# Layers 1 and 2 in program order: columns among the three-tap products, spectra taken once and copied with signs among the frequency products, group statistics in the stage before

## The chip, the cores and the metric

The kernel runs on one core of one Trainium2 chip. A core has a matrix engine (TensorE, PE in the profile, with its weight loads shown apart as PEld), a vector engine (VectorE, DVE), a scalar engine (ScalarE, ACT), a general engine (GpSimd, POOL) and a sync engine that here issues DMAs (SyncE, SP). Each engine works through a queue of its own in order, and semaphores tie the queues together. Matrix products land in PSUM, which has eight banks of 128 x 512 f32; everything else stands in SBUF, 128 partitions wide. The metric is the time of one execution on the chip in microseconds; the median of several runs is given, and one further execution is profiled.

## The reference, cut to what matters

The input x is (2, 128, 64, 64) in f32: two images of 128 channels. Four layers each add something to x, after a group normalisation with 32 groups of 4 channels:

```python
def _gn(v, G=32, eps=1e-5):          # mean and variance of 4 channels x 64 x 64
    ...
x = x + _L0_conv_ref(_gn(x), ...)    # layernorm, 1x1 to 5C, depthwise 3x3, two attentions, 1x1, layernorm, 1x1
x = x + _L1_conv_ref(_gn(x), ...)    # convolutions and a correlation over columns, below
x = x + _L2_conv_ref(_gn(x), ...)    # product of spectra, below
x = x + _L3_conv_ref(_gn(x), ...)    # attention of 8 heads over 4096 positions
```

Layer 1:

```python
xp = jnp.pad(x, ((0, 0), (0, 0), (0, 0), (6, 6)))
t1 = jnp.stack([xp[..., 2 * k:2 * k + w] for k in range(7)], axis=2)
t2 = _conv(x, w2, (0, 1))                                    # 1x3, C to C: the three taps
t3 = jnp.einsum('nakhw,nbhw->nakb', t1, x) / math.sqrt(h * w)
t4 = ...                                                     # t2 shifted by -3..3 rows
t9 = p9w * (p6w * t3)
t7 = _conv(t2, w7, (0, 2), groups=c)
t8 = _conv(x, w8, (4, 4), dilation=(2, 2), groups=c)
t10 = jnp.einsum('nakb,nakhw->nbhw', t9, t4) / math.sqrt(c * 7)
return t8 - (t10 - t7)
```

Layer 2 splits the channels in four parts of 32 (a quaternion), takes the two-dimensional real spectrum of each, multiplies at each of 64 x 33 frequencies with 32 x 32 complex matrices, combines with signs, and goes back:

```python
Xs = jnp.fft.rfft2(xs, s=(64, 64), axes=(-2, -1))
Ws = jnp.stack([kr_w + 1j * ki_w, kr_x + 1j * ki_x, kr_y + 1j * ki_y, kr_z + 1j * ki_z])
C = jnp.einsum('piohw,qbihw->pqbohw', Ws, Xs)
Pw = C[0, 0] - C[1, 1] - C[2, 2] - C[3, 3]
Px = C[0, 1] + C[1, 0] + C[2, 3] - C[3, 2]
Py = C[0, 2] - C[1, 3] + C[2, 0] + C[3, 1]
Pz = C[0, 3] + C[1, 2] - C[2, 1] + C[3, 0]
o = jnp.fft.irfft2(P, s=(64, 64), axes=(-2, -1))
```

So part r of the result takes, with each part p of the weights, part r XOR p of the spectrum, with a sign that depends on r and p.

## The kernel before

**Order.** x stays in SBUF as `X`, 128 channels x 2 images x 4096 positions, from the first layer to the last. Instructions are written in Python; a framework assigns buffers, adds the waits that the buffers demand, and may move an instruction ahead of others of its engine by its own idea of what is due. The context `_in_order(tc)` takes that freedom away: within it each instruction of PE, DVE, ACT and POOL follows the one written before it on its engine. Before the change layer 1, layer 3, and the convolutions, the start and the end of layer 0 stand in it; layer 2 does not. Where two streams of work are to mix, one is a Python generator that is stepped between the steps of the other. DMAs are issued by SP, in their order.

**Statistics.** `_group_stats` (L123 to L143) has eight `bn_stats` on DVE, one per 512 positions, `bn_aggr`, a PE product with a 128 x 128 averaging matrix for the means (L130), three small DVE operations, a second product for the variances (L138), a square root on ACT (L140) and a reciprocal on DVE. Another form, `_group_stats_pow` (L1200 and on), takes the power -1/2 on POOL instead; layers 0 and 3 use it. Both are called at the start of the layer whose input they describe.

**Layer 0.** `normalize(b)` (L1289) normalises an image in eight tiles of 512 positions: ACT applies the group normalisation, PE transposes, `spread` takes the variance over channels on DVE (L1277, L1279), a maximum and an addition on DVE (L1196) and a power on POOL (L1197), and `scaled` multiplies on DVE (L1286). `finish(b)` (L1616) does the like at the end of the layer, with the output products (L1625, L1630) and the addition to `X` (L1641). In both, `scaled` of one tile stands ahead of `spread` of the next in program order. `convolutions` (L1440) computes pointwise (L1339) and depthwise (L1361) convolutions in eight parts n = 0 to 7; for the second image, `finish` of the first is stepped within its parts 0 and 1. Copies from PSUM are shared out in turn between ACT and DVE (`in_place`, L1372).

**Layer 1.** `padded(b)` computes statistics and normalises an image into a padded frame `g`. `columns(g)` gathers eight columns of `g` at a time (ACT, L569), transposes them (PE, L572) and copies them to `xt` (ACT, L577); `convolved(g)` does the three taps (PE, L590, copied by ACT, L597); `correlated(xt)` is 64 products for `t3` (PE, L605, the record count in the chain). The order is both images padded, columns 0, taps 0, columns 1, correlation 0, taps 1, correlation 1. Then `on_tiles` (PE, L644) and `combined` (PE, L673) are worked through for each image, while DVE adds the taps of the dilated 5 x 5 convolution (L625).

**Layer 2.** Its front goes over 16 groups of four columns of each image: DVE normalises (L147), PE transposes (L774), ACT copies (`gt`, L780), PE multiplies with the matrix `fwd_h`, DVE copies to `y` (L793). `y` holds the transform along rows for 33 frequencies m, both images. The products go over eight blocks `kb` of four frequencies m each. A block has a direct half (rows 4 kb + 1 to 4 kb + 4 of the weights) and a mirror half (the rows at the other end of the spectrum, whose spectra are taken from the same transform). For each half two weight tiles of 2.1 MB are loaded (`rows_of_weights`, five buffers), and `products` does, for 33 frequencies, four partition-wide products with the real and four with the imaginary weights, of 16 columns each (L875; 264 in a half, two matmul records each), into two PSUM banks, copied out as `pz` (L885). What is multiplied is `e`, one tile for a half: at partition block p, row m, result part r, image b, it holds spectrum part r XOR p with its sign. `spectra(kb)` fills both tiles of a block: for each m and image one 128 x 512 product with the constant `perm`, a matrix of 1 and -1 that transposes, permutes and signs in one (PE, L819); a copy of 128 x 512 (`yt`, ACT, L827); four products of 128 x 198 (PE, L842); four copies of 128 x 198 (DVE, L851). `turned` (L897, L904) transposes `pz` of a half; `back` (L920, L923) takes a block back along columns. They and `spectra` of the next block are generators: `alongside(products, side, steps)` steps them between the 33 frequencies of a half. Because the layer is not in `_in_order`, the profile shows the spectra in one bunch rather than spread. At last the layer goes back along rows, 16 groups for each image (L982, L988, an addition to `X`).

**Layer 3** starts with loads of small constants on SP and statistics; its `folded(0)` prepares weights for image 0.

Of the kernel before, what the change touches and what calls it, by code (L numbers as in the profile page):

```python
# [29 lines left out]
def _blocks():  # L30
# [13 lines left out]

    sign = np.array([[1, -1, -1, -1], [1, 1, 1, -1], [1, -1, 1, 1], [1, 1, -1, 1]], f8)
    perm = np.zeros((128, 4, 4, 32))
    for r in range(4):
        for p in range(4):
            for i in range(32):
                perm[(r ^ p) * 32 + i, r, p, i] = sign[r, p]  # L50
    k["perm"] = perm.reshape(128, 512)
# [451 lines left out]


# [4 lines left out]
def _layer1(ctx, tc, X, a, cst, eps5):  # L509
# [20 lines left out]
    nc.sync.dma_start(p9.rearrange("p k c -> p (k c)"), a["L1_conv_p9w"].to_broadcast([128, 7 * C]))  # L530
    d7 = one.tile([128, C], F32, name="d7")
# [14 lines left out]
    def padded(b):  # L546
# [3 lines left out]
        mean, rstd = _group_stats(nc, two, bank, x, cst, eps5)  # L550
# [5 lines left out]
        for c in range(NCH):  # L556
            r = slice(c * ROWS, (c + 1) * ROWS)
            _normalized(nc, g[:, 4 + c * ROWS : 4 + (c + 1) * ROWS, 4 : W + 4], xi[:, r, :], mean, rstd)
        return g

    def columns(g):

        xt = two.tile([128, 32 + 6, C], F32, name="xt")
        nc.gpsimd.memset(xt[:, 0:3, :], 0.0)
        nc.gpsimd.memset(xt[:, 35:38, :], 0.0)
        for u in range(0, 32, 4):
            gw = two.tile([128, 8, H], F32, name="gw")
            w0 = 4 + 2 * u
            nc.scalar.copy(gw, g[:, 4 : H + 4, w0 : w0 + 8].rearrange("p h w -> p w h"))  # L569
            pt = bank()  # L570
            for i in range(4):
                nc.tensor.transpose(  # L572
                    pt[:, i * 128 : (i + 1) * 128],
                    gw[:, 2 * i : 2 * i + 2, :].rearrange("p w h -> p (w h)"),
                    ident,
                )
            nc.scalar.copy(xt[:, 3 + u : 7 + u, :].rearrange("p u c -> p (u c)"), pt)  # L577
        return xt

    def convolved(g):  # L580
# [5 lines left out]
        for c in range(NCH):  # L586
# [11 lines left out]
        return t2  # L598
# [94 lines left out]
    xt = [columns(g[0])]  # L693
    t2 = [convolved(g[0])]
    xt.append(columns(g[1]))
    t3 = [correlated(xt[0])]
    t2.append(convolved(g[1]))
    t3.append(correlated(xt[1]))
    some(taps(0, g[0]), 42)
    t9 = [weights(*x) for x in t3]  # L700
    rest = taps(1, g[1])
    for b in range(B):
        for c in range(NCH):
            if c % 4 in (0, 2) and c < 4:
                z = on_tiles(g[b], t2[b], c // 2)
                some(rest, 4)
            ps = combined(t9[b], t2[b], c)
            some(rest, 2)
            added(b, c * CH, ps)
            if c in (1, 3):  # L710
                added(b, c // 2 * S // 2, z)

# [4 lines left out]

def _skewed(first, second, n, depth=1):

    waiting = []  # L720
    for i in range(n + depth):
        if i < n:
            waiting.append((i, first(i)))
        if i >= depth:
            second(*waiting.pop(0))
# [3 lines left out]
def _layer2(ctx, tc, X, a, cst, src, eps5):  # L729
    nc = tc.nc  # L730
    one = ctx.enter_context(tc.tile_pool(name="l2_one", bufs=1))
    wpool = ctx.enter_context(tc.tile_pool(name="l2_w", bufs=5))
# [26 lines left out]
    with tc.tile_pool(name="l2_a", bufs=3) as ap, tc.tile_pool(  # L759
        name="l2_aps", bufs=4, space=PSUM  # L760
    ) as aps:
        for b in range(B):
            x = X[:, b, :]
            xw = x.rearrange("p (h w) -> p w h", w=W)
            mean, rstd = _group_stats(
                nc, ap, lambda: aps.tile([128, CH], F32, tag="pt", name="ps_stat"), x, cst, eps5
            )

            def columns(i):
                g = ap.tile([128, 4, H], F32, name="g")  # L770
                _normalized(nc, g, xw[:, 4 * i : 4 * i + 4, :], mean, rstd)
# [8 lines left out]
                nc.scalar.copy(gt, pt[:, :256])  # L780
# [1302 lines left out]
```

## Time and profile before

| what | value |
|---|---|
| runs | 4671.17, 4682.22, 4674.94, 4677.45, 4668.28 us |
| median | 4674.94 us |
| profiled execution, own time | 4674.02 us |
| its span | 4672.2 us |
| mean granted TensorE clock | 0.931 of full |
| PE busy | 4295.3 us, 92% |
| ACT busy | 3265.4 us, 70% |
| DVE busy | 2118.6 us, 45% |
| POOL busy | 59.3 us, 1% |
| layer 0, by its last addition to X | 0 to 1682.7 us |
| layer 1, front (statistics to the last correlation) | 1682.7 to 1851.9 us |
| layer 1, tile convolutions and combinations, to the last on PE | 1851.9 to 1984.7 us |
| layer 2, front | 1985.4 to 2030.5 us |
| layer 2, block 0 to its direct products | 2030.5 to 2063.4 us |
| layer 2, mirror half 0 to direct half 7 | 2063.4 to 2542.3 us |
| layer 2, the rest | 2542.3 to 2649.6 us |
| layer 3 | 2649.6 us to the end |

The page has the busy time of every engine, the span in 40 slices with a digit for the busy tenths in each, the granted clock of PE and the DMA's share, and the chain of work that ended last, followed back from the last instruction. Further views list single instructions in order of time, with start and duration in microseconds, the engine, the line of the kernel, the operation, output and inputs, and in square brackets how long the engine was idle before and what released it. "x" counts records, and a piece of the chain can hold several. In the chain "issue" is time in which an engine waited for nothing that the profile shows.

### The profile page before, as it was taken

The page shows a single profiled execution, that of the slowest core. Times are in us where ns is not written, and L with a number is a line of the kernel's source. Part 1 is how long each engine was busy: PE and PEld are TensorE (multiplying, and loading weights), DVE is VectorE, ACT ScalarE, POOL GpSimd, SP SyncE. Part 2 cuts the span into 40 slices and gives each one's busy share as a digit, 9 for nine tenths or more (in the row PEclk, how much of TensorE's full clock was granted, in tenths as well). Part 3 has the DMA queues.
Part 4 walks back from the last instruction along what each step waited for, and adds up shares of the span by engine and source line. Part 5 has one row for each costly group of instructions (what it writes and reads, how often), then busy time and mean ns, then how long its engine had stood idle before and what let it go on. Part 6 is the DMA issues. An engine that isn't in the chain of part 4 may idle for free.

```text
span 4672.2 us, 95822 instructions
## 1 busy us (share of the span) xinstructions
PE 4295.3 (92%) x42698; PEld 1789.4 (38%) x42698; DVE 2118.6 (45%) x2192; ACT 3265.4 (70%) x3735; POOL 59.3 (1%) x141
## 2 busy tenths in 40 slices
PE   7899999889999968977676899999999999999998
PEld 3522222452222234466566733333333333333332
DVE  3689999458999986851121321131113211221111
ACT  3478888438888822221011289999999999999998
POOL 1000000000000010000000000000000000000000
PEclk9999999999999979986676589999999999999999
DMA  1000000000000000089876000000000000000000
GB/s 44 2 1 1 1 1 1 1 2 1 1 1 1 1 6 1 1 136 140 124 122 87 7 3 6 6 6 4 6 6 6 6 6 6 6 6 6 6 6 4
DMA packets 154267, 90.60 MB, mean 19 GB/s; under 512 B 24297, under 2 KB 148201, under 8 KB 153842
## 3 DMA queue, kind: packets, MB, share of 16 engines
q1 hardware_dynamic: 153842, 84.36, 11.1%
q8 instruction: 337, 5.52, 0.5%
q14 instruction: 88, 0.72, 0.1%
HBM read 75.94 MB, written 4.19 MB: 17 GB/s over the span
## 4 chain that ended last, share of the span: by engine, by line
PE 85%; DVE 6%; issue 5%; ACT 3%; POOL 1%; DMA 0%; SPq 0%; DVEq 0%; ACTq 0%; POOLq 0%
PE ps_acc L1884 22%; PE ps_s L1865 18%; PE ps_s L1166 12%; PE ps_acc L1570 11%; PE ps_sp L1361 3%; PE ps_freq L875 3%; PE ps_bank L673 2%; PE ps_pe L842 2%; PE ps_bank L819 1%; DVE sums L1605 1%; PE ps_t L605 1%; PE ps_sp L1339 1%; PE ps_po L994 1%; PE ps_bank L590 1%; PE ps_acc L1819 1%
## 5 line engine op out<-in xcount | busy, mean ns | idle before, releaser
L1875 ACT ACTIVATE weights<-ps_s 128x1024 f32<-128x1024 f32 x2048 | 1888.2, 1094 | 65.8 <-PE ps_s L1865 63.0
L1175 ACT ACTIVATE weights<-ps_s 128x1024 f32<-128x1024 f32 x1024 | 992.5, 1022 | 173.4 <-PE ps_s L1166 148.3
L1884 PE MATMUL ps_acc<-weights,vt 128*32 128x512 f32 x8192 | 1095.6, 607 | 0.0
L1865 PE MATMUL ps_s<-q,k 32*128 32x512 f32 x8192 | 933.1, 446 | 10.3 <-ACT weights L1875 10.3
L1605 DVE TENSOR_TENSOR sums<-sums,weights 128x2048 f32<-128x2048 f32 x384 | 879.1, 2289 | 42.4 <-ACT weights L1175 6.4
L1865 PEld LDWEIGHTS ps_s<-q,k 32*128 32x128 f32 x8192 | 473.8, 183 | 851.4 <-ACT weights L1875 792.1
L1166 PE MATMUL ps_s<-q,k 32*128 32x512 f32 x4096 | 646.2, 642 | 2.7 <-ACT weights L1175 1.3
L1570 PE MATMUL ps_acc<-weights,vt 128*32 128x512 f32 x4096 | 548.8, 605 | 3.4 <-ACT used L1595 3.2
L1906 DVE COPY u<-ps_acc 128x512 f32<-128x512 f32 x32 | 22.1, 692 | 1069.9 <-PE ps_acc L1884 1069.9
L1166 PEld LDWEIGHTS ps_s<-q,k 32*128 32x128 f32 x4096 | 210.0, 183 | 429.5 <-issue 212.4
L1884 PEld LDWEIGHTS ps_acc<-weights,vt 128*32 128x32 f32 x8192 | 163.1, 108 | 379.2 <-issue 367.2
L1570 PEld LDWEIGHTS ps_acc<-weights,vt 128*32 128x32 f32 x4096 | 81.0, 108 | 395.1 <-issue 377.0
L875 PE MATMUL ps_freq<-e,w_r 128*32 128x16 f32 x4224 | 143.4, 220 | 69.8 <-issue 69.4
L875 PE MATMUL ps_freq<-e,w_i 128*32 128x16 f32 x4224 | 141.4, 220 | 71.7 <-issue 71.7
L625 DVE SCALAR_TENSOR_TENSOR X<-g,w,X 128x2048 f32<-128x2048 f32 x84 | 197.3, 2350 | 2.4
L1605 DVE TENSOR_TENSOR sums<-weights 128x2048 f32<-128x2048 f32 x64 | 146.5, 2289 | 59.8 <-ACT weights L1175 59.8
L1361 PE MATMUL ps_sp<-pad,diag 32*32 32x512 f32 x4608 | 166.8, 607 | 4.0 <-DVE q L1372 3.3
L875 PEld LDWEIGHTS ps_freq<-e,w_r 128*32 128x32 f32 x4224 | 135.0, 159 | 76.3 <-issue 75.4
L875 PEld LDWEIGHTS ps_freq<-e,w_i 128*32 128x32 f32 x4224 | 134.2, 159 | 75.6 <-issue 75.5
L885 ACT COPY pz<-ps_freq 128x272 f32<-128x272 f32 x16 | 6.8, 424 | 213.0 <-PE ps_freq L875 213.0
L1826 DVE TENSOR_TENSOR vt<-ps_acc,bv 128x384 f32<-128x384 f32 x32 | 17.9, 558 | 295.4 <-PE ps_acc L1819 295.4
L885 DVE COPY pz<-ps_freq 128x256 f32<-128x256 f32 x16 | 6.8, 425 | 279.4 <-PE ps_freq L875 207.7
(278 smaller groups left out, 3200.9 us busy)
## 6 DMA issues: line engine op xcount, KB each, us to landing
w_r<-in_L_conv_kr_w SPq DMA_DIRECT2D x15, 528.0 KB, 12.1
w_r<-in_L_conv_kr_x SPq DMA_DIRECT2D x15, 528.0 KB
w_r<-in_L_conv_kr_y SPq DMA_DIRECT2D x15, 528.0 KB, 11.9
w_r<-in_L_conv_kr_z SPq DMA_DIRECT2D x15, 528.0 KB, 11.8
w_i<-in_L_conv_ki_w SPq DMA_DIRECT2D x15, 528.0 KB, 6.0
w_i<-in_L_conv_ki_x SPq DMA_DIRECT2D x15, 528.0 KB, 8.2
w_i<-in_L_conv_ki_y SPq DMA_DIRECT2D x15, 528.0 KB, 11.1
w_i<-in_L_conv_ki_z SPq DMA_DIRECT2D x15, 528.0 KB, 12.7
```

Source lines behind the costliest of these rows:

```text
L625: nc.vector.scalar_tensor_tensor(xi, g[:, i : i + H // 2, j : j + W], w8[:, s : s + 1], xi, ALU.mult, ALU.add)
L673: nc.tensor.matmul(ps.rearrange("p (h w) -> p h w", w=W), t9[:, k, :], t2[:, c * ROWS + k : (c + 1) * ROWS + k, 2 : W + 2], start=(k == 0) ...
L842: nc.tensor.matmul(pe[:, j * 6 * FW : j * 6 * FW + n * 3 * FW], yt[:, (r + j) * 128 : (r + j + 1) * 128], fwd_w[:, : n * 3 * FW], start=Tr ...
L875: nc.tensor.matmul(out.rearrange("p (x c) -> p x c", c=2), ws[n][:, :, s * FW + fw], e[:, s, :, :, 1 - n : 3 - n, fw].rearrange("p r b e - ...
L1166: nc.tensor.matmul(ps[j // 2][:, j % 2, :], k[rows, kt * 128 : (kt + 1) * 128], q[rows, qb * CH : (qb + 1) * CH], start=True, stop=True,)
L1175: nc.scalar.activation(w[:, 2 * p : 2 * p + 2, :], ps[p], AF.Exp)
L1361: nc.tensor.matmul(ps[r // 2][to, r % 2, :].rearrange("p (h w) -> p h w", w=W), diag[rows, grp, t, :], pad[rows, y0 : y0 + ROWS, t % 3 : t ...
L1570: nc.tensor.matmul(ac[n][rows, :], lhs(rows), w[:, j, :], start=first, stop=last)
L1605: nc.vector.tensor_add(parts[0].rearrange("p j c -> p (j c)"), t.rearrange("p j c -> p (j c)"), w.rearrange("p j c -> p (j c)"),)
L1865: nc.tensor.matmul(ps[j // 2][:, j % 2, :], k[rows, kt * 128 : (kt + 1) * 128], q[n][rows, qb * CH : (qb + 1) * CH], start=(n == 0), stop= ...
L1875: nc.scalar.activation(w[p], ps[p], AF.Exp)
L1884: nc.tensor.matmul(ac[0][32 * j : 32 * j + 32, :], vt[:, kt, j // 2, i : i + 2, :].rearrange("p a d -> p (a d)"), w[j // 2][:, i, :], star ...
```

## The change

Five things are changed together.

1. Layer 2 is put into `_in_order`. `spectra` drops the matrix `perm`: for each m both images are transposed into one bank, copied once (128 x 256), multiplied with `fwd_w` (two products of 128 x 198), and then copied 32 times (16 where only one half is wanted), a block of 32 partitions by 198 elements each, from part r XOR p to partition block p of `e`, with the sign as a factor: on ACT where p is even, on DVE where p is odd. Each r (four p) is a step of the generator, woven among the products of the mirror half. Of block 0 only the direct half's spectra are made ahead; the mirror half's are stepped among the direct products.
2. The front of layer 2 normalises on ACT with a scale and a shift, and copies `gt` on DVE.
3. Layer 1's `columns` and `convolved` become one function: gather group c + 1, then the three taps of row group c and the transposes of column group c.
4. The statistics of a layer's first image are computed in the layer before, as steps of a generator: layer 1's in layer 0's second convolutions, layer 2's among layer 1's combinations for the second image, layer 3's in the way back of layer 2. All use the power on POOL, so the square root on ACT goes. Layer 2's second image is stepped among the column groups of the first.
5. In layer 0's `normalize` and `finish`, `spread` stands ahead of `scaled`.

The diff, cut to its core:

```diff
 def _layer1(...)
+        if b or st is None:
+            st = two.tile([128, 2], F32, tag="st", name="st")
+            for _ in _stats_steps(nc, two, bank, x, cst, mhalf, st):
+                pass
...
-    def columns(g):
+    def columns_and_convolved(g):
...
+        def gathered(c):
+            gw = two.tile([128, 8, H], F32, name="gw")
+            w0 = 4 + 8 * c
+            nc.scalar.copy(gw, g[:, 4 : H + 4, w0 : w0 + 8].rearrange("p h w -> p w h"))
+            return gw
+
+        def worked(c, gw):
             ps = bank()
             ... # three taps of row group c, as before
             nc.scalar.copy(t2[:, 3 + c * ROWS : 3 + (c + 1) * ROWS, 2 : W + 2], pv)
-        return t2
+            pt = bank()
+            for i in range(4):
+                nc.tensor.transpose(pt[:, i * 128 : (i + 1) * 128], gw[:, 2 * i : 2 * i + 2, :]..., ident)
+            nc.scalar.copy(xt[:, 3 + 4 * c : 7 + 4 * c, :].rearrange("p u c -> p (u c)"), pt)
+
+        _skewed(gathered, worked, NCH)
+        return xt, t2
...
-    xt = [columns(g[0])]
-    t2 = [convolved(g[0])]
-    xt.append(columns(g[1]))
-    t3 = [correlated(xt[0])]
-    t2.append(convolved(g[1]))
-    t3.append(correlated(xt[1]))
+    xt, t2 = zip(*(columns_and_convolved(x) for x in g))
+    t3 = [correlated(x) for x in xt]
...
             some(rest, 2)
+            some(steps, 1)
...
+        if there is not None and b == 0:
+            steps = _stats_steps(nc, two, bank, X[:, 0, :], cst, mhalf, there)
...
 def _layer2(...)
+    ctx.enter_context(_in_order(tc))
...
             def columns(i):
                 g = ap.tile([128, 4, H], F32, name="g")
-                _normalized(nc, g, xw[:, 4 * i : 4 * i + 4, :], mean, rstd)
+                nc.scalar.activation(
+                    g, xw[:, 4 * i : 4 * i + 4, :], AF.Identity, bias=shift, scale=scale
+                )
+                next(steps, None)
...
-                nc.scalar.copy(gt, pt[:, :256])
+                nc.vector.tensor_copy(gt, pt[:, :256])
...
-                nc.tensor.matmul(pt, y[:, b, m, :, :].rearrange("p c w -> p (c w)"), k["perm"], ...)
-                yt = two.tile([128, CH], F32, name="yt")
-                nc.scalar.copy(yt, pt)
+                for b in range(B):
+                    nc.tensor.transpose(
+                        pt[:, b * 128 : (b + 1) * 128],
+                        y[:, b, m, :, :].rearrange("p c w -> p (c w)"),
+                        ident,
+                    )
+                yt = two.tile([128, B, 128], F32, name="yt")
+                nc.scalar.copy(yt.rearrange("p b i -> p (b i)"), pt[:, : B * 128])
...
+                for r in range(4):
+                    for p in range(4):
+                        to, of = slice(32 * p, 32 * p + 32), slice(32 * (r ^ p), 32 * (r ^ p) + 32)
+                        for s, e, row in places:
+                            out, x = e[to, row, r], got[of, :, s]
+                            if p % 2:
+                                nc.vector.tensor_scalar_mul(out, x, float(SIGN2[r][p]))
+                            else:
+                                nc.scalar.mul(out, x, float(SIGN2[r][p]))
+                    yield
...
-        es = []
-        for _ in spectra(0, es):
+        es = [None, None]
+        for _ in spectra(0, es, (0,)):
             pass
...
-            e = list(es)
-            side = iter(())
+            e, es = es, [None, None]
+            side = spectra(0, e, (1,))
             if before:
                 side = chain(turned(before[2][1], before[1]), back(kb - 1, before[0], before[1]))
-            alongside(products(rows_of_weights(kb, False), e[0], pz), side, 8)
+            alongside(products(rows_of_weights(kb, False), e[0], pz), side, 8 if before else 20)
             side = turned(pz[0], direct)
             if kb + 1 < BLOCKS2:
-                side = chain(side, spectra(kb + 1, es))
+                side = chain(side, spectra(kb + 1, es, (0, 1)))
             alongside(products(rows_of_weights(kb, True), e[1], pz), side, 24)
...
+def _stats_steps(nc, pool, psum_tile, x, cst, mhalf, got):
+    ...
     for c in range(NCH):
         nc.vector.bn_stats(st[:, c, :], x[:, c * CH : (c + 1) * CH])
+        if c % 2:
+            yield
...
     nc.vector.bn_aggr(mv, st)
+    yield
     pm = psum_tile()
     nc.tensor.matmul(pm[:, 0:1], cst["group"], mv[:, 0:1], start=True, stop=True)
...
+    yield
     pv = psum_tile()
     nc.tensor.matmul(pv[:, 0:1], cst["group"], e, start=True, stop=True)
+    _power(nc, pool, got[:, 1:2], pv[:, 0:1], 0.0, 1e-5, mhalf)
+    yield
...
 # layer 0, normalize
+            if 1 <= c < NCH + 1:
+                r[c - 1] = spread(turned[c - 1])
             if 2 <= c < NCH + 2:
                 y[c - 2] = scaled(turned[c - 2], r[c - 2])
-            if 1 <= c < NCH + 1:
-                r[c - 1] = spread(turned[c - 1])
...
 # layer 0, convolutions(pool, b, before)
+        if b == 1:
+            later = _stats_steps(nc, small, lambda: acc(0), X[:, 0, :], cst, mhalf, there)
...
+            if n in (3, 4):
+                for _ in range(4):
+                    next(later, None)
```

## The prediction

> **What bounds the kernel now.** The page first. Layers 0 and 3, the two attentions, fill most of the span, and the change hardly touches them. The granted clock and the DMA row mark layer 2: five slices of 0.5 to 0.8 clock with the DMA at 8 to 9 tenths. The chain is PE's nearly everywhere, with 5% of "issue".
>
> ```profile
> PE   7899999889999968977676899999999999999998
> PEclk9999999999999979986676589999999999999999
> DMA  1000000000000000089876000000000000000000
> PE 85%; DVE 6%; issue 5%; ACT 3%; POOL 1%; DMA 0%; SPq 0%; DVEq 0%; ACTq 0%; POOLq 0%
> ```
>
> Second, busy time by stretch for layer 2: its front, block 0, the seven further pairs of mirror and direct half, the last mirror half, the way back.
>
> ```profile
> 1985.40:2030.50 45.10, 31.84 (x200) 27.40 (x200) 41.33 (x91) 12.45 (x34) 0.00 (x0) 0.81 1.21 190
> 2030.50:2063.40 32.90, 27.60 (x608) 22.58 (x609) 10.57 (x33) 5.14 (x9) 0.00 (x0) 0.94 0.59 90
> 2063.40:2542.30 478.90, 337.60 (x8308) 286.23 (x8308) 87.19 (x252) 56.11 (x100) 0.00 (x0) 0.68 0.83 124
> 2542.30:2570.70 28.40, 20.76 (x577) 18.67 (x577) 2.20 (x5) 2.76 (x5) 0.00 (x0) 0.62 0.01 3
> ```
>
> Columns: stretch, length, then PE, PEld, DVE, ACT, POOL busy, clock, DMA share, GB/s. A pair takes 478.9/7 = 68.4 us, in which DVE works 12.5 and ACT 8.0: both have room, if they may use it. Third, the chain through one pair. The spectra stand in one bunch, PE alone from 2203.52 to 2222.42 (18.9 us). Products come in bursts of some 2.2 us with gaps put down to "issue", although nothing they read is late:
>
> ```profile
> 2187.22 2.23 PE ps_freq L875 x118
> 2189.45 6.18 issue
> 2195.63 2.21 PE ps_freq L875 x110
> 2256.13 2.18 PE ps_freq L875 x116
> 2258.31 6.23 issue
> ```
>
> About 128 matmuls with their 128 weight loads make a burst. The gap is 6.2 us while weights stream, 1.5 us when none do (block 0). A burst's period is so 8.4 or 3.7 us, whatever PE could do, and other work put between products is covered by it. Fourth, the start of layer 1:
>
> ```profile
> 1690.24 1.28 ACT L140 ACT_TABLE_LOAD   x1 [10.78 <-PE ps_bank L138]
> 1704.89 1.11 ACT L569 COPY gw<-g 128x512 f32<-128x512 f32 x1
> 1726.90 23.23 PE ps_bank L590 x48
> 1771.78 29.68 PE ps_t L605 x64
> ```
>
> T0 = 1682.69 ends layer 0. Up to 1726.9 PE is mostly idle: statistics, then columns of image 0, bound by ACT and PE in turn.
>
> **Layer 0.** In `normalize` and `finish` POOL's power (L1197, 1.02 us) and the hand-overs to it (some 0.1) stand on the chain, each tile once. The change lets DVE scale the previous tile (0.69) meanwhile. At the start 8 tiles gain at most 0.7 each: 5.6; I take -5 (-9 to -3). The first `finish`, inside the second image's convolutions, has a 3.8 us cycle over 8 tiles, but PE's own work there is some 3.5: -4 (-6 to -1). The last: -3 (-5 to 0). New in the second convolutions are the statistics for layer 1: eight `bn_stats` are 4.8 us of DVE (L126), and two small PE products (0.6 each) wait for DVE in PE's order with the fifth depthwise convolution (at 989.88) behind them: +4.5 (3 to 8). ACT's copies are queued behind no new wait. Sum: -7.5.
>
> **Layer 1.** Now image 0 is normalised at T0 (3.74 us), then the small scalings 2.0, `bn_stats` of image 1 4.84, aggregate 0.37, and the two PE products with DVE between them 1.9: PE may start convolving at T0+13. ACT's gathers (1.03), xt copies (0.59) and t2 copies (0.59) make 2.2 us per c. Beside them PE does a c's six matmul records (23.23/8 = 2.9) and transposes (1.13 at most), 3.3 to 4.0 in all, so ACT hides: eight times 3.3 is 26.2, for the first image 2.5 more to fill; correlations 57.2 (29.68 + 27.48). That ends at T0+125; now the tile convolutions (L644) start at 1851.93 = T0+169. So -44, or -43 with copies at the ends. Statistics of layer 2 among the last image's combinations: DVE lags PE there, and two products wait some 4: +4. Layer 1: -39 (-44 to -33). It is hidden nowhere: PE runs densely from 1851.93 to 1984.7.
>
> **Layer 2, front and end.** Without statistics (some 8 us for image 0), and with the normalisation moved to ACT and the gt copies to DVE, DVE keeps two operations per step, 0.37 and 0.60. 32 steps of 0.97, the other statistics 5.5 and the arrival of the constants 4.5 give about 41 against 45.1: -5 with the shorter constants (-8 to 0). SP's queue keeps its order, constants before weights, so the first weights are not later. The statistics at the end: two PE waits, +1. Layer 3 is held by its bias loads (2655.44, 2.89 us) anyway: -0.3; its Exp table load at 2700.55 (1.28) goes: -1.3. Sum: -5.6.
>
> **Layer 2, the spectra.** PE's work falls: per pair 8 times 2.2 us of 128x512 and 128x198 matmuls (L819, L842) become 4 times two transposes and two matmuls (some 1 us). The price is copies: 32 per m, of 32x198, ACT (L890) and DVE (L888) taking turns on one PSUM bank. Neither form is in the trace. By size ACT's copy lies between 0.22 (64 elements, L1346) and 0.373 (256, L780): 0.33. DVE's 128x198 copy is 0.36 alone, 0.32 to the next (L851): a pair is 0.68. Do the engines overlap? The nearest rows read another bank in quarters, ACT and DVE in turn:
>
> ```profile
> 945.36 0.68 DVE L1372 COPY q<-ps_sp 32x512 f32<-32x512 f32 x1 [9.50 <-ACT q L1372]
> 946.07 0.58 ACT L1372 COPY q<-ps_sp 32x512 f32<-32x512 f32 x1 [0.75 <-DVE q L1372]
> 946.68 0.69 DVE L1372 COPY q<-ps_sp 32x512 f32<-32x512 f32 x1 [0.64 <-ACT q L1372]
> ```
>
> Strictly one after the other, each waiting for the other's copy, 0.03 us between. The new copies have the same pattern: one tile read, one tile written, engines alternating. So an m costs 8 x 0.66 + 8 x 0.68 + 16 x 0.03 = 11.2 us, serially; four take 45. (With ACT's ends and DVE's 0.32 or 0.36 throughout, x is 9.1 to 12.2.) They are queued behind `turned` of the direct half: first copy about 8 us into the mirror half (5 to 11: last pz copy, eight transposes 1.9, two ACT copies, a fetch gap). The next direct half needs all of them, at 8 + 45 = 53. That half has 528 matmuls (8448 records in 16 halves), 4.1 bursts of 2.2 = 9, `turned` and the way back (1.9 + 7.0) between them, two or three short gaps and pz: 22 (19 to 25). Pair: 75.0 against 68.4, +6.6 seven times: +46. PE, the weights (0.83 of 68.4 = 57 us of transfer) and the gaps all fit beneath.
>
> Block 0: sixteen copies per m serially, 6.0; four and filling 2 give 26 where 18.6 was; then the mirror's spectra beside the direct products, 24 + 2.6 against 14.4. In all 52.6 against 32.9: about +19. The last mirror half and the way back stay.
>
> The page "PSUM — Partial Sum Buffer", section "PSUM bank collisions raise a hardware error", says that two engines may access one bank at once if their 32-partition quadrants differ. The copies of different p mostly qualify; by that rule alone they could overlap, and the first rival's sum would hold. The rows above do differ in quadrant and still go in turn, which shows an ordering that the program carries; I go by the rows.
>
> **Sum.** -7.5 - 39 - 5.6 + 46 + 19 = +13, on the profiled execution's own 4674.02 us: 4687. (It is 0.9 below the median 4674.94, so nothing is corrected.)
>
> **Rivals.** *First, the other side: the copies overlap or are short.* With x for an m's copies, a pair is 30 + 4x and block 0 is 8 + 4x, so layer 2's products change by 32x - 294: at x = 11.2 it is +65; it balances the -52 elsewhere at x = 10.8 and says faster by over 0.2% below 10.5. That is 0.02 us per copy, so this rival needs little. If the engines overlap fully, x = 16 x 0.34 = 5.5; the pair then meets its transfers at 57 to 59: -9.4 x 7 - 3 - 52 = -121, 4553. For: DVE's next copy starts earlier than its record ends (0.32 against 0.36), ACT has small copies of 0.22. Against: the rows above.
>
> *Second, slower still:* with the copies stretched over the mirror half, its matmuls of the next direct half no longer run ahead of the gaps, and the direct half meets full streaming: another 6.2 us gap per pair, 7 x 6.2 = 43: 4730. For: every gap with weights in flight is 6.2. Against: PE's mirror products end early, so the weights start earlier and are mostly there.
>
> *Third, the layer-1 gain is not there:* the convolutions wait for ACT's gathers in ACT's order, 2.2 us plus PE's transposes per c, as the columns do now (2.82 per c). Then PE works as slowly as before and only the statistics go, -20 instead of -39: 4706.
>
> *Fourth, as before:* with x near 10.8, 4674.
>
> The page "Runtime: NRT & Kernel Launch", section "Instruction fetch mechanics", says instructions come in blocks of 256 and their loading is mostly hidden. The gaps after each 256 here, 1.5 and 6.2 us, are not; were they hidden, a direct half would be some 12 us shorter before and after alike.
>
> **How the numbers follow.** What is uncertain is mostly layer 2: x by 0.7 gives 22, the direct half by 3 gives 21, the first copy by 3 gives 21, the rest 8; together about 32 either way; the ends of x alone, 9.1 and 12.2, would give 4620 and 4719. My forecast's kind (serial copies, x over 10.9) 0.54, first rival 0.20 (full overlap 0.06 of it), second 0.11, third 0.08, fourth 0.07. The bounds that leave out 2 in 10 are 4630 and 4745. A difference of 0.2%, 9 us, is about what a measurement of this kernel can tell from no change. Faster by more: the first rival and the forecast's lower spread, 0.31. Within: the fourth and what lies around it, 0.17. Slower: 0.52. The forecast's own range is 4660 to 4720.
>
> **What would show it.** Right: L890 and L888 in strict turns, each idle "<-" the other's e; PE idle at the first product of a direct half until the last e copy; a pair of about 75 us; convolutions of layer 1 from T0+13 and its tile convolutions at T0+125; no table load at the start of layer 1; a PE gap of 4 us ahead of the fifth depthwise convolution of image 1. Wrong: ACT and DVE busy with e at the same instant, a pair under 68, or a PE that waits for gw in layer 1. What would upset the sum most is the price of a 32x198 copy, since 128 of them stand in each pair's chain: 0.02 us each is 20 us in all.

## The result and the profile after

| | time |
|---|---|
| before, median of 44 runs | 4675.36 us (4667.29 to 4683.29) |
| after, median of 24 runs | 4681.66 us (4674.25 to 4689.55) |
| ratio after to before | 1.0012, 95% interval 1.0007 to 1.0018 |
| forecast | 4687 us, 4630 to 4745 |

The change costs 0.12%: measurable over this many runs, and inside the band of 0.2% that the prediction had called "the same" (chance given: 0.17; "slower": 0.52). The forecast was 5 us too high. That closeness is luck: two of its steps were wrong by 40 and 37 us, with opposite signs, and 5.5 us come from a stretch whose code is the same and whose difference no run explains.

The page of the kernel after, its slices and its chain:

```profile
PE   6999999789999979955465889999999999999998
PEclk9999999999999989976656589999999999999999
DMA  1000000000000000177976000000000000000000
PE 77%; DVE 13%; ACT 6%; issue 3%; DMA 0%; SPq 0%; POOL 0%; DVEq 0%; ACTq 0%; POOLq 0%
```

PE's share of the chain has gone from 85% to 77%, DVE's from 6% to 13%, ACT's from 3% to 6%: work that was PE's alone now ends on other engines. The stretches of layer 2 (columns as before: length, busy time of PE, PEld, DVE, ACT, POOL, clock, DMA share, GB/s), cut at the same events as in the prediction:

```profile
1977.40:2013.40 36.00, 29.71 (x196) 24.08 (x196) 32.42 (x81) 24.43 (x32) 0.55 (x1) 0.95 1.21 183
2013.40:2068.10 54.70, 25.07 (x585) 20.32 (x585) 23.50 (x65) 23.81 (x73) 0.00 (x0) 0.64 0.75 112
2068.10:2556.30 488.20, 274.66 (x7896) 232.48 (x7895) 159.14 (x477) 154.34 (x519) 0.00 (x0) 0.60 0.79 119
2556.30:2584.70 28.40, 21.64 (x578) 19.14 (x579) 2.20 (x5) 2.76 (x5) 0.00 (x0) 0.70 0.01 3
```

In the seven pairs PE is busy 63 us less than before (274.7 against 337.6), and the pairs still take 9.3 us longer (488.2 against 478.9). DVE and ACT work 72 and 98 us more.

A table by stage shows where the 6.2 us by which the profiled span is longer (4678.4 against 4672.2) come from. The events are the first or last instruction of the named lines in the two traces.

| stage | before | after | difference | forecast |
|---|---|---|---|---|
| layer 0, to the last addition to X | 1682.7 | 1715.0 | +32.3 | -7.5 |
| layer 1, to its last addition | 302.7 | 262.5 | -40.3 | -39 |
| layer 2, front | 45.0 | 35.9 | -9.1 | -5 |
| block 0, to the direct half's pz | 32.8 | 54.8 | +21.9 | +19 |
| seven pairs of mirror and direct half | 478.9 | 488.2 | +9.3 | +46 |
| last mirror half, way back | 107.8 | 108.4 | +0.6 | +1 |
| layer 3, start to its first Exp | 51.9 | 48.8 | -3.1 | -1.6 |
| layer 3, the rest and the end of the span | 1970.4 | 1964.9 | -5.5 | 0 |

### The profile page after: what moved, and what is told of

The parts are those of the page before. It is cut to its first block, busy times and chain, and to the rows that moved or that the text cites. A ratio compares the mean times of both kernels' runs of the same rounds, so it can differ in the third digit from the quotient of the medians.

```text
span 4678.4 us, 95586 instructions
## 1 busy us (share of the span) xinstructions
PE 4224.3 (90%) x42260; PEld 1731.8 (37%) x42260; DVE 2202.2 (47%) x2452; ACT 3386.2 (72%) x4212; POOL 66.1 (1%) x145
## 4 chain that ended last, share of the span: by engine, by line
PE 77%; DVE 13%; ACT 6%; issue 3%; DMA 0%; SPq 0%; POOL 0%; DVEq 0%; ACTq 0%; POOLq 0%
PE ps_acc L1953 22%; PE ps_s L1934 18%; PE ps_s L1215 12%; PE ps_acc L1636 11%; DVE X L644 4%; PE ps_sp L1420 3%; DVE e L888 3%; ACT e L890 3%; PE ps_freq L912 2%; DVE sums L1671 1%; PE ps_sp L1398 1%; PE ps_po L1032 1%; PE ps_acc L1888 1%; ACT weights L1224 1%; PE ps_bank L957 1%
## 5 line engine op out<-in xcount | busy, mean ns | idle before, releaser
L890 ACT ACTIVATE e<-ps_pe 32x198 f32<-32x198 f32 x512 | 144.1, 320 | 180.8 <-DVE e L888 163.4
L888 DVE TENSOR_SCALAR e<-ps_pe 32x198 f32<-32x198 f32 x512 | 166.6, 357 | 216.2 <-ACT e L890 216.0
L644 DVE SCALAR_TENSOR_TENSOR X<-g,w,X 128x2048 f32<-128x2048 f32 x84 | 197.3, 2350 | 2.4
## 6 DMA issues: line engine op xcount, KB each, us to landing
w_i<-in_L_conv_ki_y SPq DMA_DIRECT2D x15, 528.0 KB, 10.8
```

Of the source, the lines that this page charges most:

```text
L644: nc.vector.scalar_tensor_tensor(xi, g[:, i : i + H // 2, j : j + W], w8[:, s : s + 1], xi, ALU.mult, ALU.add)
L888: nc.vector.tensor_scalar_mul(out, x, float(SIGN2[r][p]))
L890: nc.scalar.mul(out, x, float(SIGN2[r][p]))
```

## The experiments

Each run is compared with the kernel before on the same chip. What is said of stages is from the traces, cut as in the table.

**1 and 2: the order in layer 0's `finish`.** The largest miss was layer 0. The last `finish` takes 59.3 us from the attention's last Exp to the last addition, against 43.2. Its cycle in the chain of the kernel after (start, duration, engine, what):

```profile
1671.12 0.89 DVE ln_st L1336 x4
1672.01 0.29 DVE ln_mv L1338 x4
...
1672.33 0.17 DVE ln_r L1245
1672.50 0.60 DVE y L1345
...
1673.24 0.75 PE ps_sp L1691 x4
1673.98 1.71 PE ps_acc L1696 x2
1675.69 0.43 PE ps_sp L1701 x2
...
1678.21 0.89 DVE ln_st L1336 x4
```

A tile now takes 7.1 us, and the chain goes through DVE and PE one after the other. Before, the same stretch had no PE in its cycle:

```profile
1660.95 1.02 POOL ln_r L1197
1661.99 0.69 DVE y L1286
1662.69 0.66 DVE X L1641
1663.35 0.80 DVE ln_st L1277 x4
1664.14 0.29 DVE ln_mv L1279 x4
...
1664.77 1.02 POOL ln_r L1197
```

The first experiment puts the old order back in `finish` alone, the second puts the new order alone into the kernel before.

```diff
 # experiment 1, against the kernel after (experiment 2: the reverse, against the kernel before)
-            if c < NCH:
-                r[c] = spread(ps[c])
             if 1 <= c < NCH + 1:
                 y[c - 1] = scaled(ps[c - 1], r[c - 1])
             if c >= 3:
                 ...
+            if c < NCH:
+                r[c] = spread(ps[c])
```

> The changed kernel with the order in finish put back (scaled of the tile before, the addition to X, then spread); normalize keeps its new order. Theory A, that the new order ties DVE and PE into one loop (spread of tile c waits for PE's products of c, these stand behind PE's transposes of tile c-2, which wait for a scaled that now stands behind the spread of c-1): the last finish goes from 55 us back to 39 (-16) and the first, inside the second image's convolutions, from 58.8 between its first and eighth addition back to 48 (-10.5), so 4681.7 - 26.5 = 4655. Theory B, that the lost time in layer 0 comes from the statistics newly put into the convolutions and the last finish is slow for another reason (PE's clock): no more than -5, 4677. The gap of 4 to 5 us before the fifth depthwise convolution stays in both.

> The kernel before with the new order in finish alone. Theory A: +16 in the last finish and +10 in the first, 4675.4 + 26 = 4701. Theory B (the order by itself is harmless or helps, as the prediction had it, -7): 4668 to 4675.

Measured: experiment 1 4650.2 us, ratio to before 0.9955 (0.9936 to 0.9974); experiment 2 4706.8 us, 1.0073 (1.005 to 1.0095). In experiment 1 layer 0 ends at 1687.0, 27.9 us earlier than after. Its last `finish` is 43.2 again and the first takes 49.8 instead of 58.8 from its first to its eighth addition. In experiment 2 layer 0 ends 33.0 us later than before; 16 of it in the last `finish`, 9.4 between the additions of the first, and 5.0 ahead of its first addition, which had not been counted, and 1.8 between the eighth addition and the second attention. Theory A holds from both sides: this one move costs some 28 to 34 us. Its old-order cycle, from experiment 1, has POOL's power on the chain again and is the quicker one:

```profile
1662.55 0.69 DVE y L1345
1663.24 0.66 DVE X L1707
1663.89 0.80 DVE ln_st L1336 x4
1664.70 0.29 DVE ln_mv L1338 x4
...
1665.32 1.02 POOL ln_r L1246
```

**3 and 4: the turns of ACT and DVE.** After the change every row m has its copies in strict turns. Some of them in order of time, ACT's (L890) and DVE's (L888) (start, duration, engine, line, operation, what, and in brackets the idle time and its releaser):

```profile
2242.75 0.55 ACT L890 ACTIVATE e<-ps_pe 32x198 f32<-32x198 f32 x2 [0.70 <-DVE e L888]
2244.02 0.55 ACT L890 ACTIVATE e<-ps_pe 32x198 f32<-32x198 f32 x2 [0.72 <-DVE e L888]
```

```profile
2243.33 0.65 DVE L888 TENSOR_SCALAR e<-ps_pe 32x198 f32<-32x198 f32 x2 [0.61 <-ACT e L890]
2244.59 0.62 DVE L888 TENSOR_SCALAR e<-ps_pe 32x198 f32<-32x198 f32 x2 [0.61 <-ACT e L890]
```

Each engine stands idle for as long as the other works. Experiment 3 gives all 32 copies of a row to one engine, experiment 4 gives all to DVE.

```diff
 # experiment 3
-                            if p % 2:
+                            if todo.index(m) % 2:
                                 nc.vector.tensor_scalar_mul(out, x, float(SIGN2[r][p]))
                             else:
                                 nc.scalar.mul(out, x, float(SIGN2[r][p]))
 # experiment 4
-                            if p % 2:
+                            if True:
```

> The changed kernel with the 32 signed copies of a row m all on one engine, ACT for even places in the block and DVE for odd ones, instead of ACT and DVE in turn by p. Theory A, that the turns make one chain of the copies (9.65 us per m, 38.6 per mirror half) and that this chain sets the pair: two chains run side by side, an m takes 32 x 0.32 = 10.3 us on its engine, four m take some 21 to 23; the pair goes from 70 to 55-60, where the weights' transfers (57 us per pair) stop it, -11 seven times, and block 0 loses two times 12: 4681.7 - 77 - 24 = 4581 (4570 to 4610). Theory B, that the engines can't read PSUM for these copies at once, or that instruction fetch or the transfers set the pair anyway: the period stays at 68 to 70, 4670 to 4690.

> The changed kernel with all signed copies on DVE. Theory A (in turns, two engines do no more than one): an m takes 32 x 0.32 = 10.2 us against 9.65, so +2.2 per pair, +15, and block 0's sixteen copies 5.1 instead of 5.9 per m, -6: 4681.7 + 9 = 4691 (4680 to 4700). Theory B (the engines do overlap in part): DVE alone is clearly longer, 13 us or more per m, +13 per pair, 4775 or more.

Experiment 3: 4654.8 us, 0.9962 (0.995 to 0.9974). Experiment 4: 4704.2 us, 1.0062 (1.0039 to 1.0084). In experiment 4 the seven pairs take 503.8 us, 15.6 more than after, as theory A had it: two engines in turns do hardly more than one of them alone. (The total is 13 us above its forecast and outside the range given. Block 0 did not become 6 us shorter: it takes 55.2 against 54.8. Layer 0, whose code is the same, ends 6.5 us later in that profile, and the front and layer 3 are longer by 2 and 5; such differences of 2 to 6 us between kernels in untouched stretches appear in several runs here and were not traced.)

Experiment 3 misses its forecast by 74 us. Two chains do run side by side (ACT and DVE copy into `e` at the same time for 79 us in all, against 14 in the kernel after) and block 0 falls from 54.8 to 39.8, but the seven pairs only go from 488.2 to 471.8. The chain of a mirror half with copies by row shows what has taken the place of the turns:

```profile
2209.74 0.50 PE ps_freq L912 x23
2210.24 4.09 issue
...
2216.64 1.62 PE ps_pe L874 x4
2218.26 0.73 PE ps_freq L912 x32
2218.99 4.01 issue
...
2224.19 1.63 PE ps_pe L874 x4
...
2225.85 0.62 DVE e L888 x2
...
2236.27 0.44 DVE pz L922
...
2239.59 5.55 issue
...
2248.45 5.09 issue
```

The products stand still in "issue" (experiments 6 and 7 say for what); the last spectra (L874) stand behind them in PE's order and come at 2224.2; the 32 copies of the last row follow for 10 us with nothing beside them. The direct half takes 28.1 us on average against 23.3 in the kernel after. The one shown has 29.8 with two long gaps, 5.55 and 5.09 us; in the kernel after the same half has 25.6, with one of 5.80 and one of 0.69.

**5 and 11: the spectra earlier among the products.** Experiment 5 takes experiment 3, the old order of `finish`, and steps the side work of a mirror half twice as fast. Experiment 11 is the same without the copies by row.

```diff
-            alongside(products(rows_of_weights(kb, True), e[1], pz), side, 24)
+            alongside(products(rows_of_weights(kb, True), e[1], pz), side, 48)
```

> The changed kernel with finish's old order, the copies by row (even places ACT, odd DVE), and the side steps of a mirror half stepped twice as fast (48 instead of 24 per half), so that PE's transposes and matmuls of the spectra come in the first half of the products and the copies of the last m end with the products, not 10 us behind. Theory A (in the run with copies by row the tail of the last m's copies is exposed): the mirror half falls from 40 to 31-33 us, the pair from 69.6 to 61, 7 x 8 = 56 less: 4654.8 - 27 - 56 = 4572 (4560 to 4595). Theory B (loading of PE's instructions while weights stream paces a pair, some nine blocks of 256 at some 7.5 us whatever stands between): pair 68 to 70, 4654.8 - 27 = 4628.

> The changed kernel with finish's old order and the mirror half's steps doubled, the copies still in turns. If the chain of 38.6 us per half is what counts, an earlier start gives only the time by which the first copy comes earlier, some 4 us of 12: pair 66 against 70, 4650 - 28 = 4622 (4610 to 4640). If the late weave alone was the fault, the pair falls to 61 as with copies by row: 4585.

Experiment 5: 4572.3 us, 0.9786 (0.977 to 0.9803), a version some 2% quicker than both kernels; its seven pairs take 424.8 us, 60.7 each. (That the total meets its forecast is in part luck: against experiment 3 the pairs gave 47 us and not 56, layer 0 gave 35 and not 27.) Experiment 11: 4653.3 us, 0.9959 (0.9945 to 0.9974), no gain over experiment 1 and outside both theories; its pairs take 70.9, and the expected 66 was wrong. The difference to experiment 5 is seen half by half. One mirror and one direct half, of the kernel after, of experiment 11 and of experiment 5, by stretch (columns as above):

```profile
2286.90:2331.80 44.90, 20.31 (x560) 16.26 (x560) 20.86 (x66) 20.33 (x71) 0.00 (x0) 0.61 1.00 155
2331.80:2356.70 24.90, 18.84 (x570) 17.06 (x568) 1.81 (x3) 1.57 (x3) 0.00 (x0) 0.51 0.48 74
```

```profile
2180.40:2223.80 43.40, 18.54 (x560) 15.25 (x560) 20.83 (x65) 20.30 (x71) 0.00 (x0) 0.65 0.95 148
2223.80:2251.60 27.80, 18.76 (x568) 17.02 (x568) 1.81 (x3) 1.56 (x3) 0.00 (x0) 0.50 0.57 86
```

```profile
2146.80:2177.70 30.90, 18.05 (x560) 14.90 (x560) 20.79 (x65) 20.43 (x71) 0.00 (x0) 0.72 0.95 146
2177.70:2208.50 30.80, 18.97 (x568) 17.14 (x568) 1.80 (x3) 1.56 (x3) 0.00 (x0) 0.51 0.90 139
```

With the turns the mirror half gains only 1.5 us from the earlier start, and more of the stream falls into the direct half (share 0.57 against 0.48), which grows by 3. In experiment 5 the DMA has a share of 0.95 of 30.9 and 0.90 of 30.8 us, which looks like 57 us of transfer in a pair of 61, the floor that the prediction's first rival had named (57 to 59). But a share of 1 is not the most there is: the front of layer 2 has 1.21 at 183 GB/s, against 138 over these pairs. At 183 GB/s the 8.4 MB of a pair (138 GB/s times 60.7 us) would take 46 us, an estimate from these rows. In a quarter of the time of these pairs less than 60 GB/s moves (in slices of 1 us), and SP waits there 156 us in 12 waits for products to free a buffer. So the transfers are not the bound of experiment 5.

**6 and 7: no weight stream.** Both leave out the loading of weights after block 0: the products of all blocks use block 0's weights. Experiment 6 has the turns, experiment 7 the copies by row.

```diff
+    kept = {}
     def rows_of_weights(kb, mirror):
+        if mirror in kept:
+            return kept[mirror]
         ...
+        kept[mirror] = ws
         return ws
```

> The changed kernel, in which the weights of block 0 serve for all blocks (28 of the 32 weight tiles are not loaded, so the products are of the wrong weights). The copies keep their turns. Theory A (chain of copies): the mirror half stays at 8 + 39 = 47 to 50 us; only the direct half loses its long gaps, 24.6 to 17-20: pair 66 against 70. Theory B (instruction loading while weights stream, or the transfers): the gaps of 4 to 6 us shrink to 1.5 and the pair falls to 50 or less.

> The copies by row, and the weights of block 0 for all blocks (the rest is not loaded). If what keeps the pair at 69.6 with copies by row is the loading of instructions beside the weight stream, its gaps go to 1.5 us and the pair falls to 45 to 52 (mirror 28-32, direct 17-20): 4655 - 130 = 4525. If the copies of the last m and the waits on e keep it, it stays above 62.

One run each: 4618.6 and 4507.9 us, where the kernel before has 4674.7 on that chip. In experiment 6 a mirror half takes 44.3 us on average against 46.4 with the stream, and a direct half falls to 16.4, a pair of 60.7 (66 was expected for a bound by copies, 50 or less for one by loading); in experiment 7 they are 31.4 and 16.2, a pair of 47.6 (45 to 52 was expected). The mirror half with turns takes nearly the same with and without the stream: there the chain of copies is the bound. The rest of a pair follows the stream, the gaps among the products first of all. In experiment 7:

```profile
2234.44 2.24 PE ps_freq L917 x123
2236.68 0.89 issue
```

where experiment 5, with the stream, has in its direct half

```profile
2304.77 4.99 issue
2309.76 2.18 PE ps_freq L912 x105
2311.94 6.50 issue
```

What PE waits for in a gap can be read from the DMA records of the traces, which hold the packets that bring instructions (queue q8, kind "instruction"). In the seven pairs of the kernel after there are 62 of 16 KB, one for each 256 matmuls and weight loads of PE. Each of the 24 gaps of over 2 us contains the end of exactly one, and PE goes on 1.4 to 1.8 us behind it; in the kernel before this holds for all 19 such gaps (1.2 to 1.6 us). The packet takes not much longer beside the stream (median 1.35 us, against 1.0 in experiment 7), but it starts late: in the gap of 6.50 us above it runs from 2315.50 to 2316.88, 3.6 us after the gap began. So the gaps are PE's instructions being loaded, and beside the weight stream this loading starts too late. They are not all that the stream costs: PE's busy time in a pair is 39.6 us in experiment 3 and 33.6 in experiment 7, with a granted clock of 0.58 and 0.75. Why the clock differs was not tested.

**8: layer 1's columns and taps apart again**, the statistics left in the stages before. The edit restores the functions `columns` and `convolved` and the six pieces in their old order.

```diff
-    xt, t2 = zip(*(columns_and_convolved(x) for x in g))
-    t3 = [correlated(x) for x in xt]
+    xt = [columns(g[0])]
+    t2 = [convolved(g[0])]
+    xt.append(columns(g[1]))
+    t3 = [correlated(xt[0])]
+    t2.append(convolved(g[1]))
+    t3.append(correlated(xt[1]))
```

> The changed kernel with layer 1's columns and three taps apart again, in the old order of the six pieces; the statistics stay in the stages before. If the merge carries the gain of layer 1: the tile convolutions start at T0+157 instead of T0+121, and with DVE's taps then no longer last, the layer ends 28 us later, 4681.7 + 28 = 4710 (4700 to 4715). If the statistics carry it, +10 or less, 4692.

Measured 4719.4 us, 1.01 (1.0083 to 1.0117). (4700 to 4715 was expected; layer 0 ends 5 us later here, again untraced.) Layer 1 takes 293.9 us against 262.5 after and 302.7 before; the tile convolutions start at T0+157.9 (T0 is the end of layer 0 in each kernel). So of the 40 us gained in layer 1, 31 are the merge and 9 the statistics.

**9: the old spectra in the new order.** Old `spectra` with the permutation product, woven into the mirror half's products, all else as in experiment 1 (block 0's spectra ahead in one piece, as before).

```diff
-        def spectra(kb, es, halves):
+        def spectra(kb, got):            # as in the kernel before: L819, L827, L842, L851
...
-            side = spectra(0, e, (1,))
+            side = iter(())
```

> The changed kernel with finish's old order, and with the spectra of the kernel before (one signed permutation product, one copy and four products for each row and image, four copies on DVE) as steps among the mirror half's products in program order. If the weave itself was worth having and only the 32 copies in turns ate it: PE's 17.6 us per pair lie between products whose bursts wait for instructions, no copy chain is last, a pair takes 60 to 63 us against 70, block 0 again 33 + 6: 4654 - 20 - 60 = 4574 (4565 to 4590). If the pair is set by the loading of instructions beside the weight stream whatever is woven in, 68 to 70 us remain: 4634.

Measured 4589.2 us, 0.9826 (0.9809 to 0.9843): pairs of 64.1 us, between the two theories and nearer to the first, and a block 0 of 36.4 (32.8 before). So the weave was worth about 4 us a pair against the bunch (68.4), and the signed copies in turns spent it; the permutation product, heavier for PE, is 61 us quicker in all than the signed copies in turns (experiment 1, 4650.2).

**10: the statistics in layer 0's second convolutions spread wider**, on top of experiment 5.

```diff
-            if n in (3, 4):
-                for _ in range(4):
+            if 3 <= n <= 6:
+                for _ in range((4, 1, 1, 1)[n - 3]):
                     next(later, None)
```

> The version with finish's old order, copies by row and the mirror half's steps doubled, and in the second convolutions of layer 0 the steps of layer 1's statistics spread over n = 3 to 6 (bn_stats; aggregate; first product; second product), not over 3 and 4. If the 3 to 5 us between the eighth addition to X and the second attention are PE's wait for the statistics, they go: 4572 - 4 = 4568. If they are DVE's extra work itself, nothing moves: 4572.

Measured 4569.0 us, 0.9777 (0.9761 to 0.9793). From the eighth addition to the second attention it takes 117.0 us where experiment 5 has 120.2 and the kernel before 117.1: the 3 us were PE's wait. The total is not told apart from experiment 5's 4572.3 by these intervals.

## Why the prediction came out as it did

**Layer 0: wrong in sign.** The step that failed is "The change lets DVE scale the previous tile (0.69) meanwhile", with "-4 (-6 to -1). The last: -3 (-5 to 0)" for `finish`. It counted POOL's power as covered and left out who waits for the delayed `scaled`. In `finish`, PE's next products stand in PE's order behind the transposes of the tile that `scaled` writes, and `spread` of the next tile waits for those products. With `spread` first, `scaled` of c-1 waits for the products of c, and the products of c+1 wait for `scaled` of c-1. DVE and PE then work in turns: 7.1 us a tile instead of 3.8. Experiments 1 and 2 show it from both sides. In `normalize`, where no such PE work stands between, the move gained 1.9 us over its tiles at the start (24.4 to 22.5) against the 5 forecast. The statistics in the second convolutions were put at +4.5. The stretch is 4.8 us longer in the kernel after, but 1.8 of this the new `finish` costs without any statistics (experiment 2); with the old `finish` they cost 3.2 (experiment 1).

**Layer 1: right in total.** PE starts the taps at T0+13.1 (forecast T0+13) and the tile convolutions at T0+120.8 (forecast T0+125, against T0+169). But the end did not move by that 48: after the front, DVE's taps are last, and what follows the start of the tile convolutions is 8 us longer. The taps (L644) are 67% of the chain from 1835 to 1980. Near its end stands:

```profile
1957.91 2.35 DVE X L644
...
1960.69 0.56 PE ps_bank L1260 x2
1961.25 9.15 PE ps_bank L692 x14
```

84 of these taps are 197 us of DVE, and in DVE's order they begin only when the second image is normalised. The prediction had put only +4 there, for the statistics' products (L1260, which do wait), and not named DVE as next in line. Of the rivals, the third (no gain in layer 1) is excluded: the taps and transposes of both images took 50.4 us.

**Front, way back, start of layer 3: right within some 4 us.** The load of the Exp table at the start of layer 3 and the one in layer 1 are gone.

**Spectra: mechanism right, price too high.** Strict turns within a row, the first copy 5.4 to 11.7 us into the mirror half (forecast 8, 5 to 11), and a direct half that waits for the last copy: all as drawn, and DVE and ACT waited for each other 216 and 163 us in all.

```profile
L912 PE MATMUL ps_freq<-e,w_r 128*32 128x16 f32 x4224 | 152.0, 222 | 168.8 <-DVE e L888 109.3
...
L890 ACT ACTIVATE e<-ps_pe 32x198 f32<-32x198 f32 x512 | 144.1, 320 | 180.8 <-DVE e L888 163.4
L888 DVE TENSOR_SCALAR e<-ps_pe 32x198 f32<-32x198 f32 x512 | 166.6, 357 | 216.2 <-ACT e L890 216.0
```

The term mis-sized is "8 x 0.66 + 8 x 0.68 + 16 x 0.03 = 11.2 us" for a row. A single copy was forecast well (ACT 0.32 for 0.33, DVE 0.36 for 0.36), but the second copy of an ACT pair starts 0.23 us after the first, so a pair is 0.55 and not 0.66, and DVE's is 0.64. A row takes 9.65 us, four 38.6 instead of 45. With that x, the prediction's own formula (30 + 4x) gives 68.6 for a pair; measured were 69.7, since the direct half took 23.3 on average and the mirror half 46.4. So the second rival (one more gap of 6.2 us in each direct half, 4730) did not come. Block 0, where the copies go singly and no pair can overlap, came out at 54.8 (forecast 52.6).

The first rival put the turn of the sum at x = 10.8, so x = 9.65 is on its side, and without the loss in layer 0 the kernel is faster by 0.45% (experiment 1). What the rival did not get right is full overlap, and its floor: in experiment 3 two free chains alone give 16 us over seven pairs, since the products' gaps and the late weave are next; experiment 5, with 60.7, comes near its 59, but not because of the transfers.

Three smaller slips of the prediction changed little. Block 0's 52.6 against 32.9 is +19.7 and not +19. The four spreads 22, 21, 21 and 8 make 38 and not 32, if they are added by their squares, as independent errors are. And not every gap beside the weights is 6.2 us: in the pairs of the kernel before, the gaps of over 2 us go from 2.4 to 6.3.

The page "PSUM — Partial Sum Buffer" of the Trainium skill, section "PSUM bank collisions raise a hardware error", lets two engines work on different quadrants of a bank at once. No run here shows copies of one bank overlapping; by the rows above each engine's idle time ends with the other's semaphore, so the turns come from waits that the program carries, and copies of two banks (experiment 3) ran side by side. The page "Runtime: NRT & Kernel Launch" of the Trainium skill, section "Instruction fetch mechanics", has the loading of instructions mostly hidden. Here the gaps after each 128 products and 128 weight loads were up to 6.5 us beside the weight stream and 0.9 to 1.2 us without it, each long one with an instruction packet in it, and a pair fell from 67.4 to 47.6 us with the stream gone (experiments 3 and 7); so the measurement decides against it for streams of such short matmuls.

**Open.** After its first Exp, layer 3 is 6 us shorter in nearly all kernels with the changed layers (1948 against 1954 us in the kernel before and in experiment 2; 1952 in experiment 4), though its code there is the same; some 2 of it fall in the first eighth of image 0. No run was made to settle it. Without this difference the change would have cost 12 us and not 6.

## What to carry to other kernels

An order written out by hand is a set of waits: before an operation is moved ahead of another on one engine, ask which engine waits for the one that falls behind, and whether the one moved ahead waits for that engine in turn. Copies that two engines make in turns out of one tile are one chain, about as long as one engine's work alone; give each engine a source tile of its own (in experiment 3 both still write the same `e`). And when the chain is cut, look at once for what is next (here the instruction loading beside a weight stream, and where in the program order the side work stands), because two changes that gave some 24 us and nothing alone gave some 80 together, each run taken against the kernel before on its own chip. And a DMA share near 1 is no proof of a bound: look for a stretch of the same kernel that moves more.

## What was not expected of the hardware

The length of a half whose work is the same changes with the weight stream beside it, but not by the stream's share alone. At a granted clock of 0.50 to 0.51 a direct half took 24.9 us at a DMA share of 0.48, 27.8 at 0.57, 29.7 at 0.62 and 30.8 at 0.90; in experiment 9, at a clock of 0.64, it took 28.4 at a share of 1.01. With no stream it took 15 to 19 us, at clocks of 0.59 to 0.92. Two ACT copies of 32x198 that follow each other without a wait take 0.55 us, 0.09 less than twice their recorded 0.32.
